# A state-space and attention hybrid on one core: new prices for TensorE's work in the planner that orders the queues

## The chip, the cores and the metric

The kernel runs on one core of a Trainium2 chip. The metric is the device time of one launch in microseconds (us). Before the change three runs gave 3870.85, 3890.63 and 3907.89 us; the median is 3890.63 us. The engines are named as in the profile: PE is TensorE, DVE is VectorE, ACT is ScalarE, POOL is GpSimd and SP is SyncE, which issues most of the transfers (DMAs).

## What is computed

The input x has 4 images (batches) of 384 channels and 32 x 32 positions, all in 32-bit floats. There are two layers.

Layer 0 is a two-dimensional selective scan. After a group norm, every image is read in 4 directions (rows, columns, and both backward). For each direction, channel and one of 16 states, a recurrence runs over the 1024 positions:

```
dt = softplus(W_dt (W_x u) + bias)
h  = h * exp(dt * A) + (dt * u) * B
y  = sum over the 16 states of h * C
```

The four results are merged, normalised over the channels, passed through a GELU and added to x.

Layer 1 works on the 1024 tokens of each image: attention with 6 heads, causal and with a window of 64 positions, and then a mixture of 4 experts of which each token takes 2. An expert is a layer of 384 to 1536 with GELU and one back to 384. Both parts have a layer norm before them and are added to their input.

## The kernel before

**The scan.** A tile holds 128 rows, made of 32 channels by 4 states, and 1024 positions. There are 16 turns (image and direction), 3 channel tiles of 128, 4 blocks of 32 channels in each and 4 groups of states: 768 slots. In each slot POOL multiplies dt*u by B into one of 7 buffers z (`times_b`, line 814), ACT makes the decays dA (`decay`, 830), DVE runs the recurrence (`scan`, 856), and the product with C is made on POOL or on DVE, whichever is further behind by the planner's clocks (line 863). Then TensorE sums the states: for each pair of slots, `fold_y` (890) issues four matmuls of 512 columns with the stationary matrix `fold` of 128 rows and 32 columns; each writes another 32 rows of the same bank. They accumulate over the four state groups, and each pair's z buffers are given back once its matmuls are issued. `time_steps` (764) makes dt with a short projection: a matmul with 12 rows and 512 columns (line 779), then a chain on ACT and DVE.

**Layer 1.** When an image's scan is finished, `tokens` (967) treats it in 8 tiles of 128 tokens: norms, transposes, queries, keys, values, scores, output projection and the router's logits. `route` (1212) sorts the tokens by expert, in two parts for each image. Each image then needs 19 expert tiles of 128 tokens. For a tile, `hidden` (1390) issues 4 calls of 9 matmuls (128 columns) into `ps_hid`, ACT makes the activations `hs`, and `output` (1435) issues 4 calls of 3 wide matmuls (384 columns) into `y_ff`. The weights, 8 pieces of 576 KB, are fetched again for each tile (`w_sb`). `combine` (1464) gathers each token's two results, adds the experts' second biases by matmuls with 4 rows, and writes the output. The experts of one image thus run beside the scan of a later one; those of the last image have nothing beside them.

**What sets the order.** Each of these pieces is a Python generator that asks for one instruction, or one call of several that stay together, at a time. While the program is built, a planner (`Machine`, line 223) keeps a modelled clock for every engine, with the times at which tiles are written and read. It takes the earliest request and emits it, and so fixes the order of each engine's queue for good. `choose` (338) picks, among the requests that could start at the same time, the one with the lowest ready time plus bias:

```
best = min(able, key=lambda p: p[0] + p[1])
```

The bias is -6 us (`EARLY`) for the scan's preparations, the sums, the tokens and the routes, 0 for the decays, products and scans themselves, and +6 us (`LATER`) for the experts. Prices come from `Engine.ask` (161): for TensorE by the number of columns, the operation and the number of rows. A second number, `work`, feeds a model of TensorE's clock in `account` (270)[...].

```
[...]
```

The prices are used only while the program is built. On the chip, the engines wait for each other by semaphores, and every queue follows its emitted order.

Of the kernel before, what the change touches and what calls it, by code (L numbers as in the profile page):

```python
# [17 lines left out]
P = 128  # L18
# [118 lines left out]
class Engine:  # L137
# [23 lines left out]
    def ask(self, op, a, k):  # L161
        aps = [v for v in list(a) + [v for n, v in k.items() if n not in ("out", "accum_out")] if hasattr(v, "tensor")]
        if "out" in k:
            outs, ins = [k["out"]], aps
        else:
            outs, ins = aps[:1], aps[1:]
        if op == "value_load":
            outs, ins = [], aps
        if op == "tensor_tensor_reduce":
            outs, ins = outs + ins[-1:], ins[:-1]  # L170
        if k.get("accum_out") is not None:
            outs = outs + [k["accum_out"]]
        for v in list(k.values()):
            if isinstance(v, bass.IndirectOffsetOnAxis):
                ins = ins + [v.ap]
        n = max(v.free_size() if callable(v.free_size) else v.free_size for v in (outs if op == "matmul" else outs + ins))
        size, table = 0, None
        if "dma" in op:
            size = max(_nbytes(v) for v in outs + ins[:1])
            if op == "indirect_dma_start":  # L180
                size = P * D * 4
            cost = dict(pool=1.0, act=0.38, sp=0.48)[self.name]
        elif self.name == "pe":
            cost = max(n, 122) * (0.00088 if op == "transpose" else 0.00176)
            if outs[0].shape[0] == 32:
                cost = 0.01 + 0.00022 * n
            if ins[0].shape[0] < 32:
                cost *= 0.6
        elif self.name == "act":
            cost = 0.08 + 0.00085 * n + 0.1 * sum(hasattr(k.get(v), "tensor") for v in ("bias", "scale"))  # L190
            cost += 0.19 if "accum_out" in k else 0.0
            table = TABLES.get(a[2]) if op == "activation" else None
        elif self.name == "pool":
            cost = 0.1 + 0.0022 * n
        elif self.name == "sp":
            cost = 1.5
        else:
            cost = 0.17 + 0.00198 * n if "scan" in op else 0.14 + 0.00105 * n
            if n < 256 and not any(v.space == PSUM for v in outs + ins):
                cost += 0.5  # L200
        asked = Op(self.name, outs, ins, cost, table, size)
        if self.name == "pe":
            asked.work = cost * min(ins[0].shape[0], P) / P if outs[0].shape[0] > 32 else 0.5 * cost
        return asked


def _nbytes(ap):
    n = 4
    for s in ap.shape:
        n *= s  # L210
    return n
# [1386 lines left out]
```

## Time and profile before

| | |
|---|---|
| median of the runs | 3890.63 us |
| profiled execution | 3882.5 us |
| its span, first to last instruction | 3880.8 us |
| PE busy | 3033.4 us (78%) |
| weight loads on PE | 1841.7 us (47%) |
| DVE busy | 2940.7 us (76%) |
| POOL busy | 2824.4 us (73%) |
| ACT busy | 2226.8 us (57%) |
| mean granted TensorE clock | 0.822 |

The profile is of one execution. A group of instructions is named by its line, engine, operation and tiles; `L159` and `L148` are lines of the planner's own helpers, through which every instruction goes, so the tile's name tells what the instruction is: `ps_y<-z,fold` are the sums over states, `ps_dt` the short projection, `ps_hid` and `y_ff` the experts' two layers, `dA` the decays or the scan that writes over them. (A few transposes of the tokens also write a tile named `ps_y`; they read `yl`.) One matmul of the program appears as two instructions of the profile, a transpose as one. Idle time before a group is put down to what ended it.

### The profile page before, as it was taken

To read this page: it belongs to the slowest core of one execution; us is meant where nothing else is said; L and a number is where in the kernel's file an instruction comes from. 1 tells how busy PE (TensorE), PEld (TensorE's weight loads), DVE (VectorE), ACT (ScalarE), POOL (GpSimd) and SP (SyncE) were. 2 spreads that over 40 slices of the span, in tenths; PEclk is the share of its full clock that TensorE was granted. 3 is DMA by queue.
4 is the path that set the end of the run, shared out by engine and by line. 5 is a ranking of instruction groups with operands and counts; after the bars stand their busy time and mean duration, and the time that the engine had idled before them with its cause. 6 is when DMAs were issued, how large, how long until landed. Compare 5 with 4: busy or idle time off the path is not lost. (4 is left out here: it accounts for less than half of the span.)

```text
span 3880.8 us, 50273 instructions
## 1 busy us (share of the span) xinstructions
PE 3033.4 (78%) x15868; PEld 1841.7 (47%) x15868; DVE 2940.7 (76%) x3358; ACT 2226.8 (57%) x4017; POOL 2824.4 (73%) x1474
## 2 busy tenths in 40 slices
PE   2555555577697988777768889899787899998997
PEld 1100010045464555344345545566555557876886
DVE  2999999998888998888888899988788992332001
ACT  2545454467586777755557767778675763432221
POOL 1999989988898877888888699889787981012001
PEclk6555556678798999876678989899898999998997
DMA  5775775544478998734357989776568975459995
GB/s 202 266 273 204 270 268 203 174 143 149 171 253 333 341 374 324 285 127 164 112 208 254 329 301 347 270 254 213 203 228 295 388 272 184 136 167 327 318 318 182
DMA packets 394145, 953.65 MB, mean 246 GB/s; under 512 B 49620, under 2 KB 173400, under 8 KB 393880
## 3 DMA queue, kind: packets, MB, share of 16 engines
q1 hardware_dynamic: 385688, 925.27, 68.1%
q0 software_dynamic: 8192, 25.17, 1.9%
q8 instruction: 126, 2.06, 0.2%
q14 instruction: 139, 1.14, 0.1%
HBM read 786.39 MB, written 182.78 MB: 250 GB/s over the span
## 5 line engine op out<-in xcount | busy, mean ns | idle before, releaser
L148 POOL TENSOR_TENSOR z<-dts,bc 128x1024 f32<-128x1024 f32 x768 | 1792.9, 2359 | 186.7 <-PE ps_y L159 105.8
L148 ACT ACTIVATE dA<-dts,a 128x1024 f32<-128x1024 f32 x768 | 854.6, 1118 | 536.8 <-DVE z L148 512.1
L159 PE MATMUL ps_y<-z,fold 128*32 128x512 f32 x3072 | 725.8, 765 | 436.2 <-POOL z L148 237.2
L148 DVE TENSOR_TENSOR_SCAN dA<-dA,z 128x1024 f32<-128x1024 f32 x409 | 935.6, 2288 | 93.2 <-ACT dA L148 77.7
L148 POOL TENSOR_TENSOR z<-z,bc 128x1024 f32<-128x1024 f32 x359 | 841.7, 2355 | 110.8 <-DVE z L148 96.2
L148 DVE TENSOR_TENSOR_SCAN z<-dA,z 128x1024 f32<-128x1024 f32 x359 | 807.8, 2276 | 31.6 <-ACT dA L148 28.6
L159 PEld LDWEIGHTS ps_hid<-xbt,w_sb 128*128 128x128 f32 x5472 | 667.0, 198 | 137.2 <-issue 38.3
L159 PE MATMUL y_ff<-w_sb,hs 128*128 128x384 f32 x1824 | 680.8, 515 | 58.5 <-ACT hs L159 46.4
L159 PE MATMUL ps_hid<-xbt,w_sb 128*128 128x128 f32 x5472 | 692.0, 284 | 33.1 <-ACT hs L148 8.2
L148 DVE TENSOR_TENSOR z<-dA,bc 128x1024 f32<-128x1024 f32 x409 | 499.1, 1220 | 13.8 <-DVE dA L148 0.5
L159 PEld LDWEIGHTS ps_y<-z,fold 128*32 128x32 f32 x3072 | 93.1, 120 | 872.8 <-POOL z L148 412.8
L148 ACT ACTIVATE hs<-ps_hid,bb 128x128 f32<-128x128 f32 x912 | 274.1, 365 | 391.8 <-PE ps_hid L159 320.2
L159 PEld LDWEIGHTS y_ff<-w_sb,hs 128*128 128x128 f32 x1824 | 341.3, 199 | 314.9 <-issue 65.9
L148 POOL DMA_INDIRECT cb<-ysdr,idx x64 | 62.6, 979 | 293.7 <-DMA ysdr<-yb 269.8
L159 POOL TENSOR_TENSOR rn<-rn,half 128x1 f32<-128x1 f32 x96 | 52.7, 549 | 266.7 <-DVE rn L159 209.0
L148 DVE COPY yb<-y_ff 128x384 f32<-128x384 f32 x22 | 12.2, 556 | 251.5 <-PE y_ff L159 204.9
L148 POOL DMA_INDIRECT xsdr<-tks,idx x64 | 65.2, 1018 | 146.5 <-DVE idx L159 58.4
L148 ACT ACTIVATE ed<-ps_dt,dtb_sb 128x512 f32<-128x512 f32 x192 | 125.8, 681 | 67.6 <-PE ps_dt L148 59.8
L148 PE MATMUL ps_dt<-xd,dtw_sb 12*128 12x512 f32 x192 | 136.7, 822 | 24.7 <-DMA dtw_sb<-in_dtw_dram 14.2
L148 DVE TENSOR_TENSOR ps_dt<-ps_dt,ed 128x512 f32<-128x512 f32 x192 | 132.6, 690 | 12.3 <-ACT ps_dt L148 9.5
L148 ACT COPY ed<-ps_dt 128x512 f32<-128x512 f32 x96 | 56.0, 584 | 124.8 <-DVE ed L148 124.5
L304 ACT ACT_TABLE_LOAD x80 | 102.6, 1283 | 2.2 <-PEq L1583 0.8
(204 smaller groups left out, 3411.2 us busy)
## 6 DMA issues: line engine op xcount, KB each, us to landing
w_sb<-wl SPq DMA_DIRECT2D x608, 576.0 KB
dts<-dtr SPq DMA_DIRECT2D x384, 512.0 KB
bc<-xdr SPq DMA_DIRECT2D x128, 512.0 KB
dtr<-ed SPq DMA_DIRECT2D x192, 256.0 KB
ub<-udr SPq DMA_DIRECT2D x48, 512.0 KB
yp<-ydr SPq DMA_DIRECT2D x96, 256.0 KB
ydr<-yp SPq DMA_DIRECT2D x96, 256.0 KB
wl<-in_w_dram SPq DMA_DIRECT2D x32, 576.0 KB
```

The lines of the kernel that those rows point to most:

```text
L148: return getattr(self.real, op)(*a, **k)
L159: getattr(self.real, op)(*a, **k)
L304: self.nc.scalar.add_instruction(mybir.InstLoadActFuncSet(name=self.nc.get_next_instruction_name(), act_func_set_id=EXP_LN_SET,))
```

## The change

Only the prices in `Engine.ask` change; no instruction of the program is added, removed or altered.

```
         elif self.name == "pe":
-            cost = max(n, 122) * (0.00088 if op == "transpose" else 0.00176)
+            cost = max(n, 122) * (0.00096 if op == "transpose" else 0.0018 if n < 256 else 0.00195)
             if outs[0].shape[0] == 32:
-                cost = 0.01 + 0.00022 * n
-            if ins[0].shape[0] < 32:
-                cost *= 0.6
+                cost = 0.01 + 0.00047 * n
...
         if self.name == "pe":
-            asked.work = cost * min(ins[0].shape[0], P) / P if outs[0].shape[0] > 32 else 0.5 * cost
+            asked.work = cost * min(ins[0].shape[0], P) / P if outs[0].shape[0] > 32 else cost
```

Here n is the number of columns, `outs[0].shape[0] == 32` picks out the sums over states, and `ins[0].shape[0] < 32` matmuls over few rows. A sum's price goes from 0.123 to 0.251 us and its work from half its price to all of it; matmuls over few rows lose their reduction of 40%; matmuls of 256 columns and more rise by 11%, shorter ones by 2%, transposes by 9%.

## The prediction

> **What bounds the kernel now.** I read the slices of the page first, then busy time by stretch, then the waits, then the order of time on TensorE. The page's rows of 40 slices (97 us each, tenths busy) show two regimes.
>
> ```profile
> PE   2555555577697988777768889899787899998997
> DVE  2999999998888998888888899988788992332001
> POOL 1999989988898877888888699889787981012001
> PEclk6555556678798999876678989899898999998997
> ```
>
> VectorE (DVE) and GpSimd (POOL) carry the scan up to slice 33; from there to the end only TensorE (PE) is full. The table by stretch gives sizes (columns: stretch, length, busy us and instructions of PE, weight loads, DVE, ACT, POOL, then TensorE's clock, DMA share, GB/s).
>
> ```profile
> 100.00:800.00 700.00, 378.64 (x933) 59.56 (x933) 685.32 (x482) 340.58 (x395) 667.39 (x297) 0.57 0.68 236
> ...
> 1000.00:1650.00 650.00, 557.69 (x3063) 343.05 (x3060) 574.86 (x532) 466.91 (x807) 553.84 (x265) 0.92 0.83 305
> 1650.00:2000.00 350.00, 257.42 (x1143) 141.71 (x1142) 306.50 (x384) 203.31 (x373) 302.62 (x157) 0.68 0.43 146
> 2000.00:2750.00 750.00, 641.48 (x3676) 415.77 (x3677) 648.42 (x764) 537.57 (x979) 654.00 (x338) 0.91 0.78 273
> 2750.00:3209.00 459.00, 396.42 (x2280) 261.82 (x2278) 392.65 (x366) 306.78 (x555) 402.23 (x200) 0.92 0.79 284
> 3209.00:3560.00 351.00, 330.54 (x2159) 270.51 (x2155) 112.98 (x449) 138.96 (x376) 46.26 (x77) 0.97 0.59 192
> ```
>
> Until 800 us DVE is 98% busy and TensorE half idle: no expert work exists yet. With 800 to 1000 us (not shown), TensorE is busy 2005 of the 2409 us from 800 to 3209 (83%), DVE 2092 (87%) and POOL 2079 (86%): neither of the two is full, so they wait on something. The last sum over states starts at 3208 us. After it lie 672 us in which TensorE is 95% busy: about 7 expert tiles left from batch 2 and batch 3's tokens and 19 expert tiles.
>
> The waits of DVE and POOL between 800 and 3209 us (who waits for whom: total us, times, longest):
>
> ```profile
> POOL z L148 <- PE ps_y L159: 100.7, 47, 5.4
> ...
> DVE dA L148 <- ACT dA L148: 72.8, 58, 5.2
> DVE yp L148 <- PE ps_y L159: 28.3, 23, 3.2
> DVE z L148 <- ACT dA L148: 28.2, 23, 3.6
> ```
>
> In the same window, ACT's row for the hidden layer in the view of groups (busy us, mean ns, then idle time before it and what ended it):
>
> ```profile
> L148 ACT ACTIVATE hs<-ps_hid,bb 128x128 f32<-128x128 f32 x603 | 182.6, 365 | 130.2 <-PE ps_hid L159 107.0 <-issue 18.5 <-DMA bc<-xdr 1.0
> ```
>
> POOL loses 100.7 us because the sums that free its z buffers come late. DVE's thirteen entries for PE add to 99.6 us; it loses another 101 us (72.8 + 28.2) to decays that ACT issues late, and ACT had stood 107 us before hidden-layer results of PE. So about 200 us of DVE's 317 idle us there point to a TensorE that is later than the order expected.
>
> [...] a group of four sums takes 1.94 us in the scan-only stretch (granted clock 0.57) and 1.07 us later. [...] the eight instructions of a group have a median of 617 ns each, yet take 1.07 us together. [...] In the tail, loads are 77% busy (270.51 of 351)[...].
>
> **The change, part by part.** It changes no instruction's own duration. It changes the prices by which the greedy planner decides the order of each queue. So I compare old and new prices with TensorE's timeline (start, length, operation, instructions):
>
> ```profile
> 301.75 1.94 PE L159 MATMUL ps_y<-z,fold 128*32 128x512 f32 x8 [0.38 <-POOL z L148]
> ...
> 3025.59 1.12 PE L148 MATMUL ps_dt<-xd,dtw_sb 12*128 12x512 f32 x2 [0.40 <-DVE cb L148]
> ...
> 3116.13 2.10 PE L159 MATMUL y_ff<-w_sb,hs 128*128 128x384 f32 x6
> 3118.16 1.07 PE L159 MATMUL ps_y<-z,fold 128*32 128x512 f32 x8
> 3119.15 2.27 PE L159 MATMUL ps_hid<-xbt,w_sb 128*128 128x128 f32 x18
> ```
>
> A program matmul shows as two instructions. Per call, warm, in us:
> - **Sums over states** (4 matmuls): old 4 x (0.01 + 0.00022 x 512) = 0.49, new 4 x 0.2506 = 1.00, trace 1.07. Cold, times 1.9: old 0.93, new 1.90, trace 1.94. Off by a factor of two, now right.
> - **Short projection** (12 rows): old 0.54, new 1.00, trace 1.12.
> - **Output layer** (3 wide matmuls): old 2.03, new 2.25, trace 2.10 to 2.20. I take 2.15: it goes from a little low to a little high.
> - **Hidden layer** (9 matmuls): old 2.03, new 2.07, trace 2.27: hardly moved.
> - **Expert bias** (3 matmuls with 4 rows): old 0.41, new 0.69, trace 0.93. Transposes rise 9%, the value and x projections 11%: a few us in all.
>
> Unbooked time in 800 to 3209, from that stretch's instruction counts (sums 2272/8 = 284 groups, short 65, output 1182/6 = 197, hidden 3618/18 = 201, bias 16): old 284 x 0.57 + 65 x 0.58 + 197 x 0.12 + 201 x 0.24 + 16 x 0.52 = 162 + 38 + 24 + 48 + 8 = 280 us; new 284 x 0.07 + 65 x 0.12 - 197 x 0.10 + 201 x 0.20 + 16 x 0.24 = 20 + 8 - 20 + 40 + 4 = 52 us. The planner believed that TensorE had some 230 us more room than it had.
>
> **Work weight.** Sums now count 1.00 per group toward the modelled clock instead of 0.25[...]. A group comes every 700/100 = 7 us in the scan-only stretch[...]. Priced at nothing there. Beside other work the model warms sooner; its effect is bounded by pricing every group of the 350-us stretch at clock 0.68 (84 decays, so 42 groups) at the wrong speed: 42 x 0.9 = 38 us either way.
>
> **Where the stall goes.** I let half of the 200 us of DVE's stalls vanish, since four fifths of the error is corrected (230 of 280), but lumps stay (hidden-layer runs of up to 54 instructions, 6.3 us, cannot be interrupted). Of those 100 us the next wait takes half: DVE waiting for POOL and ACT, POOL already 86% busy. So the scan ends 50 us earlier, bounds 0 and 150. Next, TensorE has less time before the tail. From 800 to 2000 us a shorter scan gives nothing back, as TensorE has no expert work from 1650 to 2000 anyway; in the later half it gives back up to 83%: 50/2 x 0.83 = 20 us. Net -30. The DMAs keep their number and size, but their order on SP's queue and POOL's moves too. I price that at nothing, since the loads' lead over their use hides it; POOL's waits for DMAs add to about 34 us in this window, so without that cover it is 34 us either way, which the range carries.
>
> Against the profiled execution's own 3882.5 us (its span of 3880.8 and 1.7 around it): 3882.5 - 30 = 3852.5. The median of the runs shown, 3890.6, is 8 us above the profiled one, so the forecast is 3860 us.
>
> **The rivals.**
> 1. *Another wait takes the place* (chance 0.2). For it: taken by 100 us, DMA is 93 to 97% busy from 1300 to 1600 us and 100% at 3000 to 3100, so weights may pace experts and scan alike; against it: the same table has 43% at 1650 to 2000, where POOL still waits for sums. Gain 0 to 10 us: 3885.
> 2. *Experts slip into the tail* (0.22), ending slower. Folds and projections rank ahead of experts, whose bias is +6 us; booked 230 us longer, they push expert calls back, mostly in batch 2's part after 2750 us, which TensorE can't make up later. A tile costs 17.0 us in the full tail (from 3600 to 3800: hidden 108.1/896 x 72 + output 104.1/297 x 24 = 8.7 + 8.4). The scan's 50 us pay for three tiles; at six the time is 3891 + 102 - 50 = 3943. From five and a quarter on it is over 1% slower. Against it: old bookings filled only some 70% of TensorE's stretch (2005 busy us less 280 unbooked is 72% of 2409), so there is room for the new ones.
> 3. *The whole coupling goes* (0.13). If all 200 us of stalls vanish and 150 reach the scan's end, 50 given back: 3791. Against it: sums in 1650 to 2000, with no experts beside them, still held POOL 15 us.
>
> The change does reach the order: every sum carries its price, so "nothing happens" is no case.
>
> **How the numbers follow.** Forecast 0.45, rivals 0.20, 0.22, 0.13. The forecast's own range is 3830 to 3890. One percent (39 us, about what a measurement of this kernel can tell; three runs spread from 3871 to 3908) puts the bounds at 3852 and 3929. Faster by over 1%: rival 3 and half of the forecast, 0.35; slower: rival 2 and some of the work weight's loss, 0.25; the same 0.40. The range of 8 in 10 reaches into rivals 2 and 3: 3795 to 3942.
>
> **What would show it.** POOL's wait for the sums falls from 100.7 to about 50 us, ACT's wait for the hidden layer from 107 to about 70, DVE from 800 us to the last sum rises from 87 to 89%, and the last sum starts near 3158 us. The tail stays at 670 to 700 us. It is wrong if the last sum moves earlier but the tail grows by as much (rival 2), if the stall on sums stays (rival 1), or if DVE's busy time itself grows because fewer products go to POOL.

## The result and the profile after

The changed kernel takes 3826.20 us (median of four runs, 3821.22 to 3834.42) against 3889.43 us before: the estimated ratio is 0.9845, with a 95% interval of 0.9818 to 0.9873 (the two medians alone give 0.9837, which is inside it). Its profiled execution took 3821.22 us, with a span of 3819.5 us; before it was 3880.8 us, so the span is 61 us shorter. The forecast was 3860 us: the direction was right, the gain of 63 us is a little over twice the forecast's 30.

The page's rows of 40 slices (95 us each now; tenths busy) keep their two regimes:

```profile
PE   2555545578797899877678788898898989998998
DVE  2999999998889899998989989989799963321001
POOL 1999998999898887998988699898889960102001
PEclk8555556577798899996679889998898999999997
```

Busy time by stretch in the changed kernel (stretch, length, then PE, weight loads, DVE, ACT and POOL, TensorE's clock, DMA share, GB/s). The last sum over states starts at 3118.9 us, so the second row is the stretch in which the scan and layer 1 run side by side, and the last one is the tail:

```profile
100.00:800.00 700.00, 381.34 (x935) 60.59 (x931) 687.64 (x485) 341.75 (x399) 661.74 (x294) 0.55 0.68 236
800.00:3119.00 2319.00, 1957.58 (x10836) 1229.91 (x10836) 2083.70 (x2327) 1633.78 (x2960) 2071.89 (x1055) 0.88 0.74 260
1000.00:1650.00 650.00, 561.60 (x3023) 345.29 (x3024) 582.37 (x546) 472.41 (x806) 566.23 (x275) 0.91 0.84 306
1650.00:2000.00 350.00, 256.81 (x1269) 148.44 (x1269) 314.93 (x409) 220.95 (x410) 318.18 (x172) 0.73 0.52 172
3119.00:3820.00 701.00, 644.95 (x4061) 525.64 (x4057) 130.02 (x476) 219.16 (x637) 64.03 (x96) 0.94 0.71 236
```

The same view of the kernel before, from 800 us to its last sum:

```profile
800.00:3208.00 2408.00, 2004.19 (x10999) 1263.63 (x10999) 2092.47 (x2335) 1651.33 (x2990) 2079.34 (x1058) 0.87 0.71 253
```

Until 800 us hardly anything moved. From there to the last sum the scan took 2319 us instead of 2409. DVE's busy time is nearly the same (2084 against 2092 us), but its idle time fell from 317 to 235 us: 90% busy instead of 87%. The tail grew from 672 to 701 us. So the gain is 90 us in the scan, less 29 us given back in the tail.

The waits of POOL and DVE from 800 us to the last sum, in the changed kernel (total us, times, longest):

```profile
POOL z L148 <- PE ps_y L159: 32.2, 23, 5.4
...
DVE dA L148 <- ACT dA L148: 53.8, 39, 4.6
DVE z L148 <- ACT dA L148: 14.4, 16, 2.8
...
DVE ed L148 <- ACT ps_dt L148: 12.8, 8, 3.0
...
DVE yp L148 <- PE ps_y L159: 9.5, 12, 1.4
...
DVE sums L148 <- ACT s L148: 1.1, 3, 0.7
```

Two of these in the kernel before, where the prediction does not show them:

```profile
DVE ed L148 <- ACT ps_dt L148: 25.4, 20, 2.9
...
DVE sums L148 <- ACT s L148: 13.5, 8, 2.8
```

POOL's wait for the sums is a third of what it was (100.7 us). DVE's entries for PE add to 83.0 us (99.6 before), and its waits for late decays to 68.2 us (101.0). Together that is 49 us less. DVE's other waits for ACT shrank too: in the making of dt (`ed`, after ACT has added 1 to the exponential) from 25.4 to 12.8 us, for the sums of the softmax from 13.5 to 1.1 us.

The view of groups for ACT shows that its wait for hidden-layer results hardly moved (107.0 before):

```profile
L148 ACT ACTIVATE hs<-ps_hid,bb 128x128 f32<-128x128 f32 x582 | 176.2, 364 | 108.9 <-PE ps_hid L159 94.8 <-issue 8.7 <-DMA bc<-xdr 1.5
```

A stretch of TensorE's timeline in the changed kernel (start, length, operation, instructions):

```profile
1411.26 2.10 PE L159 MATMUL y_ff<-w_sb,hs 128*128 128x384 f32 x6
1413.19 2.17 PE L159 MATMUL ps_hid<-xbt,w_sb 128*128 128x128 f32 x18
1415.30 1.06 PE L159 MATMUL ps_y<-z,fold 128*32 128x512 f32 x8
1416.29 2.20 PE L159 MATMUL y_ff<-w_sb,hs 128*128 128x384 f32 x6
```

The calls have their old lengths: the median of one instruction is 617 ns for the sums, 275 for the hidden layer and 486 for the output layer in both traces. Sums between expert calls stand in the prediction's lines of the kernel before too, so this stretch shows no new kind of order.

It shows something else. The lengths of neighbouring calls overlap: from start to start a call holds TensorE for 1.93 us (output layer), 2.11 (hidden layer) and 0.99 (sums); the prediction's lines give 2.03 for the output layer and 0.99 for the sums. By this reading the sums' new price of 1.00 us is right, the old price of both expert layers, 2.03, was right within 0.1 us as well, and the output layer's new one, 2.25, is 11 to 16% too high.

The order is not quite the only difference. Where a product with C is made, and when ACT loads another table of functions, also follows from the planner's clocks: 414 of the 768 products are on DVE now instead of 409, and ACT has 154 table loads of 1.28 us instead of 160. Over the 18 kernels with old or new prices that follow below, neither number goes with the time (correlations of -0.19 and 0.18).

The tail's growth is expert work that came to lie in it. Hidden-layer instructions in the tail of the changed kernel (busy us of PE, weight loads and ACT; 72 of PE make one expert tile, as 5472 in all for 76 tiles show):

```profile
3119.00:3820.00 701.00, 241.16 (x1980) 237.56 (x1980) 97.97 (x330) 0.94 0.71 236
```

The hidden layer's row in the kernel before, from 3209 us on (busy us, mean ns, idle time before it):

```profile
L159 PE MATMUL ps_hid<-xbt,w_sb 128*128 128x128 f32 x1854 | 229.8, 280 | 7.0 <-DMA w_sb<-wl 6.1 <-PE ps_hid L159 0.9
```

So the tail holds 1980/72 = 27.5 tiles, and held 1854/72 = 25.75 before. A tile takes 16.1 us there: from 3600 to 3800 us of the kernel before TensorE is busy for 199.9 of 200 us, at a granted clock of 1.00, and does 896/72 = 12.4 tiles. (The forecast's 17.0 adds lengths that overlap, 108.1 + 104.1 us in these 199.9; its 8.7 + 8.4 make 17.1.) The 1.75 tiles thus make 28 us, nearly the whole growth.

### The profile page after: what moved, and what is told of

It is laid out like the page before. It is cut to its first block, busy times and chain, and to the rows that moved or that the text cites. A ratio compares the mean times of both kernels' runs of the same rounds, so it can differ in the third digit from the quotient of the medians.

```text
span 3819.5 us, 50289 instructions
## 1 busy us (share of the span) xinstructions
PE 3009.8 (79%) x15892; PEld 1827.9 (48%) x15892; DVE 2930.5 (77%) x3341; ACT 2222.0 (58%) x4028; POOL 2812.4 (74%) x1469
## 5 line engine op out<-in xcount | busy, mean ns | idle before, releaser
L159 PE MATMUL ps_y<-z,fold 128*32 128x512 f32 x3072 | 716.1, 761 | 409.4 <-POOL z L148 230.6
L148 DVE TENSOR_TENSOR_SCAN dA<-dA,z 128x1024 f32<-128x1024 f32 x414 | 946.7, 2287 | 71.1 <-ACT dA L148 58.6
L148 POOL TENSOR_TENSOR z<-z,bc 128x1024 f32<-128x1024 f32 x354 | 831.1, 2361 | 94.3 <-DVE z L148 91.2
L148 DVE TENSOR_TENSOR_SCAN z<-dA,z 128x1024 f32<-128x1024 f32 x354 | 796.9, 2275 | 20.3 <-ACT dA L148 14.4
L159 PE MATMUL y_ff<-w_sb,hs 128*128 128x384 f32 x1824 | 689.7, 519 | 36.4 <-ACT hs L159 30.5
L159 PEld LDWEIGHTS ps_o<-v,pt 128*128 128x128 f32 (+1 forms) x720 | 98.2, 214 | 17.7 <-issue 5.1
```

The lines of the kernel that those rows point to most:

```text
L148: return getattr(self.real, op)(*a, **k)
L159: getattr(self.real, op)(*a, **k)
```

## The experiments

Two theories stood at first. **True prices**: the order is better because the planner knows what TensorE costs, and most of the gain comes from the sums, whose price was wrong by a factor of two. **A re-rolled order**: any changed price makes the planner emit another order, and whether that one is good is chance.

### One part alone

Sums over states alone, price and work weight:

```
-                cost = 0.01 + 0.00022 * n
+                cost = 0.01 + 0.00047 * n
...
-            asked.work = ... if outs[0].shape[0] > 32 else 0.5 * cost
+            asked.work = ... if outs[0].shape[0] > 32 else cost
```

> Only the sums' price (0.123 to 0.251 us) and their whole work weight; all else as before. Theory of true prices: the sums are 142 of the 228 us of newly booked time, and POOL waits for the sums, so most of the gain comes here: 3840 to 3855 us, POOL's wait for the sums from 800 us on near 35 us. Theory of a re-rolled order (any changed price gives another order, good or bad by chance): anywhere from 3820 to 3940 us, without relation to the booked time.

The same price with the old work weight (`else 0.5 * (0.01 + 0.00022 * n)`):

> Only the sums' price; their work weight stays at the old 0.061 us each. True prices: the weight matters little, so within 15 us of the run with both, 3840 to 3865 us. Re-rolled order: a time apart from the run with both by as much as from the kernel before, 3820 to 3940 us.

Only the reduction for few rows taken away:

```
-            if ins[0].shape[0] < 32:
-                cost *= 0.6
```

> Only the 40% reduction for matmuls over few rows is taken away (short projection 0.54 to 0.90 us, expert bias 0.41 to 0.68). True prices: some 30 us of newly booked time, so a gain of 0 to 15 us: 3875 to 3890 us. Re-rolled order: 3820 to 3940 us.

Only the general prices:

```
-            cost = max(n, 122) * (0.00088 if op == "transpose" else 0.00176)
+            cost = max(n, 122) * (0.00096 if op == "transpose" else 0.0018 if n < 256 else 0.00195)
```

> Only the general prices: wide matmuls 11% up, narrow ones 2%, transposes 9%; the sums and the reduction for few rows as before. True prices: the output layer goes from a little low to a little high, the rest is small: 3875 to 3900 us. Re-rolled order: 3820 to 3940 us.

Measured: sums 3911.56 us, a ratio of 1.0062 (1.0038 to 1.0085); sums' price alone 3898.92 us, 1.0036 (1.0022 to 1.0049); short 3870.72 us, 0.9959 (0.9946 to 0.9973); wide 3867.66 us, 0.9942 (0.9923 to 0.9962). The part that was to bring most made the kernel slower, with POOL's wait for the sums at 62.8 us where true prices had put it near 35. The two that were to bring little brought 0.4 and 0.6%, more than true prices had allowed them.

In the kernel with the sums' new price and weight, the scan did end earlier, at 3186.6 us instead of 3208.7. Its tail in the view by stretch, and then the hidden layer's instructions in that tail (PE, weight loads, ACT):

```profile
3187.00:3907.00 720.00, 664.46 (x4094) 541.18 (x4090) 136.71 (x494) 218.19 (x630) 64.03 (x96) 0.93 0.70 235
```

```profile
3187.00:3907.00 720.00, 252.04 (x2016) 248.49 (x2016) 100.76 (x339) 0.93 0.70 235
```

The tail is 48 us longer than before, with 28.0 expert tiles in it instead of 25.75. That is the place that the prediction's rival 2 named, in a kernel with one part of the change; 2.25 tiles at 16.1 us are 36 of the 48 us. It also speaks against the sums as the source of the gain, but one run for each part can't tell a part from chance.

### Neighbours that should change nothing

The sums' price nudged by about 5%, in the kernel before (0.00022 to 0.00021 and 0.00023) and in the changed one (0.00047 to 0.00044 and 0.00050):

> The kernel before with a nudge: the sums' price from 0.123 to 0.118 us, nothing else. True prices (good orders follow from right prices, gradually): a change of 4% in a price that is wrong by a factor of two does nothing, 3875 to 3900 us, last sum at 3200 to 3215 us. Re-rolled order (any nudge gives another order of another quality): the time moves by 15 us or more, and the last sum by as much, to either side.

> The kernel before with the sums' price nudged up from 0.123 to 0.128 us. True prices: 3875 to 3900 us. Re-rolled order: moves by 15 us or more, and not in line with the nudge down.

> The changed kernel with the sums' price nudged down from 0.251 to 0.235 us (6%), all else as changed. True prices: the changed prices stay right, so 3815 to 3840 us and a last sum at 3110 to 3130 us. Re-rolled order: the changed kernel is one good draw, and a neighbour falls back towards 3850 to 3900 us.

> The changed kernel with the sums' price nudged up from 0.251 to 0.266 us (nearer to the 0.267 us of the trace). True prices: 3815 to 3840 us. Re-rolled order: falls back towards 3850 to 3900 us.

Transposes nudged by 1%, in the changed kernel (0.00096 to 0.00095 and 0.00097) and in the one before (0.00088 to 0.00089):

> The changed kernel with transposes nudged from 0.96 to 0.95 ns a column, which hardly any work hangs on. Two parts (a mean effect of the prices plus a draw): between 3820 and 3895 us, near 3856; the last sum at 3119 to 3171 us, 30 to 120 us earlier than in any kernel with the old prices; the tail near 709 us. Pure draw (the prices mean nothing): a last sum as often after 3200 us as before it.

> The changed kernel with transposes nudged from 0.96 to 0.97 ns a column. Two parts: as the nudge down, 3820 to 3895 us with a last sum at 3119 to 3171 us. Pure draw: no such bounds.

> The kernel before with transposes nudged from 0.88 to 0.89 ns a column. Two parts: 3870 to 3905 us, near 3887; the last sum at 3205 to 3240 us, the tail near 660 us. Pure draw: as often below 3170 us as above.

Measured: 3896.55, 3878.49 and 3881.76 us around the kernel before; 3847.54, 3893.00, 3842.81 and 3843.22 us around the changed one; the kernel before, run beside them, had medians of 3885 and 3888 us. Around the kernel before, a nudge moved the time by 6 to 12 us only, less than the 15 expected of a re-rolled order, though two of the last sums moved by 20 and 32 us. Around the changed kernel it moved the time by 17 to 67 us. The worst case is the neighbour with the sums at 0.266 us. That is nearer to a sum's recorded length, 0.267, but further from the 0.25 that it holds TensorE from start to start, so this one run could also be read as the cost of a price that is too high; the nudges of transposes can't.

All four neighbours of the changed kernel are slower than it is. But four of the five kernels with new prices are faster than all four with old ones, so the prices do something too. The neighbour with transposes at 0.95 ns ended its scan outside the range expected, at 3102.9 us, and had 31 tiles in a tail of 738 us. The fifth kernel, with the sums at 0.266 us, lost its gain in a tail of 725 us with 29.25 tiles, as the hidden layer's instructions there show:

```profile
3171.00:3897.00 726.00, 259.54 (x2106) 254.83 (x2106) 104.14 (x351) 0.95 0.71 240
```

### Parts again, each with neighbours

To average the chance away, the changed kernel with the sums at their old price and weight, plain and with transposes nudged by 1% to either side:

> The changed kernel with the sums at their old price and work weight: short projections, wide matmuls and transposes new. If the sums make the earlier end of the scan: a last sum at 3180 to 3205 us and 3855 to 3880 us, as the short and wide prices alone gave. If short and wide prices do it together: a last sum at 3120 to 3150 us and 3830 to 3855 us.

> All new prices except the sums', with transposes nudged from 0.96 to 0.95 ns a column. If the short and wide prices alone carry the mean gain: near the run without the nudge and near the mean of the five kernels with all new prices, 3830 to 3865 us, with a last sum at 3140 to 3180 us and a tail of 660 to 690 us. If that run was a lucky draw and the sums' price is needed: 3865 to 3895 us.

> The same with transposes at 0.97 ns a column. Short and wide prices carry it: 3830 to 3865 us. Sums' price needed: 3865 to 3895 us.

And the sums' new price and weight alone, with transposes nudged from 0.00088 to 0.00089 and 0.00087:

> Only the sums' price and work weight new, with transposes nudged from 0.88 to 0.89 ns a column. If the sums' price by itself trades an earlier end of the scan for experts in the tail: last sum at 3165 to 3200 us, a tail of 705 to 735 us, 3885 to 3920 us. If the first run of this edit was an unlucky draw: 3840 to 3885 us with a tail below 700 us.

> The same with transposes at 0.87 ns a column. Trade: 3885 to 3920 us, tail 705 to 735 us. Unlucky draw: 3840 to 3885 us.

Measured: 3844.36, 3867.97 and 3822.31 us without the sums' price; 3875.72 and 3884.69 us with it alone. Kernel by kernel this decides nothing: of the first three one lies where short and wide prices were to carry the gain, one where the sums' price was to be needed, and one below both. The two with the sums' price alone lie where the first run was to be an unlucky draw, with tails of 690 and 665 us instead of the 705 to 735 of a trade.

The means tell more. All kernels by which prices are new (medians of runs in us, the others from the profiled executions, means over the kernels):

| prices that are new | kernels | medians of runs | mean | last sum | tail | hidden-layer tiles in it |
|---|---|---|---|---|---|---|
| none | 4 | 3889, 3897, 3878, 3882 | 3886.6 | 3220 | 662 | 25.1 |
| sums | 4 | 3912, 3899, 3876, 3885 | 3892.7 | 3190 | 701 | 27.3 |
| short, wide | 3 | 3844, 3868, 3822 | 3844.9 | 3172 | 668 | 25.9 |
| all | 5 | 3826, 3848, 3893, 3843, 3843 | 3850.6 | 3137 | 712 | 28.6 |

The short and wide prices are worth 42 us with the sums' old price (3886.6 to 3844.9) and 42 us with the new one (3892.7 to 3850.6). The sums' price costs 6 us in both pairs. A fit of both effects to all 18 kernels, `short` and `wide` counted as half each, gives -42 us (standard error 9) for short and wide, +5 us (8) for the sums, and a scatter of 17 us from kernel to kernel, if each kernel counts as an independent draw. So the sums' price has no effect on the time that these runs can tell from nothing. With `short` and `wide` as two effects, the fit gives -19 and -22 us, with a standard error of 14 each: which of the two brings the gain stays open. From start to start, the short projection's price came nearer to the trace (0.54 to 1.00 us; in the kernel before, the call after the one that the prediction shows starts 1.05 us later), while the output layer's went away from it.

The columns of the last sum and the tail say where the time goes. The sums' price ends the scan 30 to 35 us earlier and makes the tail 39 to 44 us longer. The short and wide prices end it 48 to 53 us earlier and lengthen the tail by 6 to 11 us only. These are means: the kernel with the sums' price alone and transposes at 0.87 ns shows no such trade, with a last sum at 3212.5 us and 25.0 tiles in a tail of 665 us.

A wait that the short price should ease is that of ACT for the short projection, between 800 us and the last sum. In the kernel with this price alone new:

```profile
ACT ed L148 <- PE ps_dt L148: 25.8, 30, 5.4
```

Before it was 41.0 us in 40 waits. But it is 33.3 us with the wide prices alone, so it does not single out the short one. The four kernels with old prices have 41 to 46 us there, the four with only the sums' price 35 to 55, the three with short and wide prices 21 to 35 and the five with all 19 to 30. Behind this wait stands the chain on ACT and DVE that makes dt, and DVE's wait for ACT in that chain (`ed`) fell with it in the kernels with both prices, from 25 to 26 us to between 8 and 19, but hardly with the short price alone (24.0); with only the sums' it is 12 to 23. POOL's wait for the sums falls with either edit: 99.6 us on the mean with old prices, 69.9 with the sums', 63.2 with short and wide ones, 58.2 with all. Which of these waits ends the scan earlier is not shown, as no run changes one of them alone.

### The experts' place, and the price still wrong

The changed kernel with the experts' bias lowered (`EARLY, LATER = -6.0, 3.0`), to see whether it is their rank that fills the tail:

> The changed kernel with the experts' bias lowered from +6 to +3 us. If the order of experts against the rest sets how many expert tiles are left for the tail, as the sums' price seemed to do: fewer tiles in the tail (26 or less instead of 27.5), a tail of 690 us or less, and a last sum 10 to 40 us later than 3119 us; the total between 3815 and 3860 us. If the tail follows only from when the scan ends: tail and tiles as in the changed kernel for the same last sum.

Measured: 3868.79 us, 0.9948 (0.9929 to 0.9966), with a last sum at 3140.2 us. The tail in the view by stretch, and then the hidden layer's instructions in it:

```profile
3140.00:3858.00 718.00, 668.05 (x4188) 544.08 (x4180) 131.60 (x483) 225.94 (x653) 64.05 (x96) 0.94 0.72 240
```

```profile
3140.00:3858.00 718.00, 254.22 (x2070) 249.93 (x2070) 103.22 (x348) 0.94 0.72 240
```

28.75 tiles and a tail of 718 us, with a total above the 3815 to 3860 us expected: in this one kernel, lowering the bias did not bring the experts forward. What speaks for the other reading is that over the 18 kernels the tiles in the tail go with the scan's end (correlation -0.74): on the average 3.7 tiles more for a scan that ends 100 us earlier, 60 us at 16.1 us each. That would account for some 20 us of the 39 to 44 that the sums' price adds to the tail. It is a correlation, and an order that holds experts back could itself end the scan earlier. Where the rest comes from stays open.

The short and wide prices with the hidden layer and the output layer at their recorded lengths (`else 0.00197 if n < 256 else 0.00187`):

> The short and wide prices without the sums', and in addition narrow matmuls up to the hidden layer's traced 0.252 us and wide ones down to the output layer's 0.72 us. If each price that comes nearer to the trace helps by its unbooked time (about 40 us of it here, on 200 calls): 3815 to 3840 us. If the sums' lesson holds here too (a dearer expert call only comes later): tail over 690 us, 3845 to 3880 us.

Measured: 3835.09 us, 0.9867 (0.9833 to 0.9901), a last sum at 3157.1 us, 26.5 tiles in the tail. It is inside the 3815 to 3840 us of the first expectation, but also within the scatter around the 3844.9 us of its three neighbours without that price; one kernel can't decide it. Nor does it test prices that are right from start to start: by the lines above a matmul of the hidden layer then takes 0.23 us, not 0.252, and one of the output layer 0.64 to 0.68, not 0.72. No version beat the changed kernel by more than the runs can tell: the best, 3822.31 us (all new prices but the sums', transposes at 0.97 ns), has the same ratio, 0.9845.

## Why the prediction was right and wrong

- **What bounds the kernel** held: DVE and POOL carry the work until the last sum (90 and 89% busy from 800 us to there in the changed kernel), with waits for TensorE, and TensorE is the bound after it (92% busy in the tail, DVE 19 and POOL 9).
- **The part-by-part sum failed at its main term.** It booked 142 of 228 us to the sums and 30 to the short projection, and took the gain to follow the booked time. The sums' price was off as described, and with the right one POOL's wait for the sums falls (99.6 to 69.9 us). But the four kernels with the sums' price alone are no faster on the average than those with none. The short and wide prices, 30 and 44 us by that sum, together bring the gain of 42 us. The sum also took a call's recorded length for the time that it holds TensorE: from start to start, the 24 and 48 us that it found unbooked for the output and the hidden layer shrink to 0 and some 16 (an estimate from 2.03 and 2.11 us a call), and the output layer's new price overshoots by 0.2 to 0.3 us a call. An estimate's error in us was no measure of what its correction is worth.
- **Where the stall goes** was the mis-sized term for this kernel's own gain. I let 100 us of DVE's stalls on PE vanish and half of that be taken by the next wait. Measured: those stalls fell by 49 us only, but nothing took their place; DVE's other idle time fell by another 33 us, most of it in waits for ACT. With 9 us less busy time this makes the 90 us of the scan's end, instead of 50. The step from TensorE over ACT to late decays is not borne out as written: DVE's waits for decays fell by 33 us, while ACT's wait for hidden-layer results fell by 12.
- **What is given back** was put at 20 us and is 29, by the mechanism that was named: 1.75 expert tiles more in a tail in which TensorE is 92% busy. On the mean of the five kernels with all prices new against the four with old ones it is 50 us, for 83 us in the scan.
- **A term was missing**: that a nudge of any price gives another order, and another time, with a scatter of 17 us. The mean over five kernels with the new prices is 36 us below the mean of the four with old ones, near the forecast's 30 (its four neighbours alone are 30 us below); the changed kernel itself lies 24 us under the mean of its five. That part of its gain is the draw. That the mean came near is partly luck too, as 83 - 50 stands where I wrote 50 - 20.
- **The work weight** was priced at nothing, with 38 us either way, and that was my estimate. The two kernels with the sums' price, with and without it, differ by 13 us, inside the scatter; one pair says no more. In the scan-only stretch, from 100 to 800 us, the granted clock was 0.56 in both of them, 0.57 in the kernel before and 0.55 in the changed one; one instruction of the sums has a median of 1061 ns there in the last two, against 617 over the whole trace. How much work raises the clock was not shown.
- **The signs named in advance**: POOL's wait for the sums 32 us (forecast 50), DVE 90% busy (89), the last sum at 3119 us (3158), the tail 701 us (670 to 700). ACT's wait for the hidden layer was to fall to 70 us and stayed at 95; on the mean of the four kernels with old prices and the five with all new ones it fell from 120 to 85.
- **Rival 2** did not decide the result, but its outcome, more experts in the tail, is in eight of the nine kernels with the sums' new price (tails of 690 to 738 us; the ninth has 665). That they were pushed back by the longer bookings is its reading, and not shown. Rival 1 is ruled out for this kernel, as the stall on the sums fell and the scan ended 90 us earlier. The coupling didn't go as a whole (rival 3): 151 of DVE's 201 us remain.

## What to carry to other kernels

Where a planner writes the order of the queues, a change of its prices has two effects: a mean one and another draw among orders. Measure a few neighbours with a nudged price on both sides before the gain is put down to the price; here a nudge alone was worth up to 67 us, and the part that was wrong by most brought nothing that these runs can tell. Read what a call costs a queue from start to start, as recorded lengths can overlap (here 1.93 us from start to start for a recorded length of 2.10). And split the time at the point where the bound changes: an edit that ends the first regime earlier may hand the same work to the second.

## What was not expected of the hardware

Nothing in the hardware: the sums and the experts' calls take the same time in both traces (medians of 617, 275 and 486 ns for one instruction of the sums, the hidden and the output layer). The surprise is how much nearly the same instructions in another order can differ: 3822 to 3912 us over all these kernels, none of which changes what is computed.
